# A two-layer graph-attention kernel: which queue stores the transposed rows in the first scores and the sums of h in the first aggregate

## The chip, the cores and the metric

The kernel runs on one core of a Trainium2 chip, as one program with one launch. The metric is the device time of a whole execution in microseconds (us). A core has five engines that run at once, each with its own instruction stream: TensorE (PE, matrix products), VectorE (DVE), ScalarE (ACT), GpSimd (POOL) and SyncE (SP). They wait for one another through semaphores. A transfer (DMA) between the chip's memory and on-chip memory is issued by an instruction on one of these streams and then carried out by 16 DMA engines that all streams share.

## The reference

Two layers of graph attention work on 2708 rows of 1024 values in fp32. `adj`, 2708 x 2708 integers, says which pairs of rows count.

```python
h = jnp.maximum(_layernorm(x, axis=-1), 0.0)
# layer 0
f = h @ Wf + bf
g = h @ Wg + bg
e = jax.nn.relu(f @ g.T)
scores = jnp.where(adj > 0, e, NEG)
attention = jax.nn.softmax(scores, axis=1)
x = x + attention @ (h @ W + bW)
# layer 1, on the h of the new x
h1 = h @ W1
e = jax.nn.leaky_relu(h1 @ a1 + (h1 @ a2).T, negative_slope=0.2)
attention = jax.nn.softmax(jnp.where(adj > 0, e, neg), axis=1)
x = x + jax.nn.relu(attention @ h1)
```

Only layer 0 is touched here: its scores (the argument of the softmax) and its product of the attention with h.

## The kernel before, in words

**Tiles.** The rows of h are taken in 21 tiles of 128 rows and a small rest. Twenty tiles form ten pairs, numbered 0 to 9; pair q holds tiles 2q and 2q+1. The rest is a left-over unit. The output rows are worked on in five panels of some 512 columns, numbered 0 to 4. "First" scores and "first" aggregate mean those of panel 0 in layer 0.

**Products in seven parts.** Large products are done two by two blocks at a time with seven products (M1 to M7) in place of eight. That takes sums and differences of the blocks beforehand. The left operand of the scores is h transposed, so for each pair the kernel keeps eight tiles of 128 x 512 of transposed rows: four straight from transposing and four sums of these. The right operand of the aggregate's side is h itself, again with sums of its blocks.

**The order of stages.** First a product of the weights, M = Wf Wgᵀ (line 591), while x is loaded, normalised and transposed (`make_pairs`, from line 441). Then `project_q(0)`, which makes the right sides B of the first scores, then `scores(0, B)`, then `project_q(1)` with the softmax of panel 0 beside it, then `aggregate(0, 0, ...)`, then `project` and the next panel. So TensorE does long products while VectorE and ScalarE prepare the next ones.

**Work in between.** Preparing steps are put on a list with an estimated time each (`put`, line 201). The stages call `behind(us)` at fixed places between their products, which takes steps off the list as long as their credit lasts. The steps are written into the program at that place, so their order is fixed when the program is built. VectorE is held in program order in the scores, SyncE's loads (`load`, line 137) and ScalarE's transfers through `by_scalar` (line 545) everywhere; the other instructions are ordered by a scheduler.

**The transposed rows.** For one pair, `transposes` (line 464) transposes on TensorE into psum banks; ScalarE copies four of them to four buffers `ts`, called hsT, each two tiles long (512 KB). `sums` (line 478) makes the other four tiles on VectorE, in the order M5, M6, M7, M3, and then stores the four buffers to `hs_d[q]` in the chip's memory. The store is `store` (line 141), a DMA issued by GpSimd. The buffers' order is that of `BY_SCORES` (line 31): M1 with M6, M5 with M2, M7 with M3, M4 with the last. Each store waits for the sum that lies in its buffer.

**The first scores.** `scores(p, B)` (line 1399) goes over the ten pairs q. At the start of each, `make_until(q + 2)` sees to it that pair q + 2 has been made, so that the last pairs are transposed, summed and stored while TensorE works on earlier ones; in the first scores these are pairs 7, 8 and 9 for the stores. Then `fetch(q + 3)` issues the loads of a later step's part of `adj` (tiles adj_i and, for panel 0's 64 extra columns, adj_t). `product` (line 1415) loads the left operands As from `hs_d[q]` with SyncE, two of the seven at a time, and multiplies them (line 1424). M4 of a pair comes only after the first product of the next pair, through `left_over`. VectorE adds up what TensorE leaves in psum (sx, sy, sz), and TensorE needs these banks again.

**The buffers.** hsT, As, adj_i, the tiles of h for sums (hr), and many more (hc, weights) all come from one pool, `strm`, of 12 buffers of 512 KB. A buffer is given out again when its last user is done. For an hsT buffer, that is its store to hs_d.

**The first aggregate.** `rows_h` (line 368) stores a pair's h to `hg_d`; later `sums_h` (line 376) loads it back (hr), makes the sums M5, M7, M6 and M3 on VectorE in two steps, and stores them to `hg_d` again, in three stores. Some pairs' sums are made before the aggregate, the others in it; `sums_until(NQ)` after product M4 makes the rest. The loads are ScalarE's or SyncE's. The aggregate (line 678) goes over its products in the order M1, M2, M4, M5, M6, M3, M7, and ScalarE copies what M1 left in psum (gx) to on-chip tiles.

**Completion semaphores.** In the built program, DMAs that SyncE and ScalarE issue report to eight completion semaphores, taken in turn in the order in which the program was written; GpSimd's report to eight others. A DMA that takes a semaphore carries a wait for the last DMA on it.

**Another transfer in that time.** `columns_to_row` (line 272) turns a few columns of r into a row in the chip's memory, `r_d` for panels 1 to 4 (called at the end of the first panel's loop body, but issued by GpSimd as soon as r is there).

Of the kernel before, what the change touches and what calls it, by code (L numbers as in the profile page):

```python
# [25 lines left out]
M1, M5, M6, M7, M3, M2, M4 = range(7)  # L26
# [31 lines left out]
def kernel(  # L58
# [82 lines left out]
    def store(o, i):  # L141
        for a, b in in_16(o, i):
            nc.gpsimd.dma_start(a, b)  # L143
# [9 lines left out]
    hs_d = [dram.tile([P, 8, NH, P], FP, name=f"hs_d{q}") for q in range(NQ)]  # L153
# [3 lines left out]
    hg_d = [dram.tile([P, 7, len(g), W], FP, name=f"hg_d{i}") for i, g in enumerate(groups)]  # L157
# [39 lines left out]
    later, lazy, credit = [], [], [0.0]  # L197
    ahead = [5]
    spare, from_slots = [False], [False]

    def put(us, go, fetch=None, takes_psum=False, ready=None, to=later):
        to.append([us, fetch, go, takes_psum, ready])
# [168 lines left out]
        for m, h in ((M1, ha[0]), (M5, ha[1]), (M2, hb[0]), (M4, hb[1])):  # L371
            store(hg_d[i][:, m, j], h)

    summed, sums_may = [0], [True]

    def sums_h():

        def fetch(q, two):
            i, j = group_of[q]
            for m in (M1, M2):  # L380
                two.append(stream("hr", (P, 2, W)))
                (load if "m" in got else by_scalar)(two[-1], hg_d[i][:, m:m + 2, j])

        def first(q, two):
            (a0, a1), (b0, b1) = ((t[:, 0], t[:, 1]) for t in two)
            add(b1, a1, b1)
            sub(a1, a0, a1)

        def second(q, two):
            (a0, a1), (b0, b1) = ((t[:, 0], t[:, 1]) for t in two)  # L390
            sub(a0, b1, a0)
            sub(b0, b0, a0)
            i, j = group_of[q]
            store(hg_d[i][:, M6:M7 + 1, j], two[0])
            store(hg_d[i][:, M3, j], b0)
            store(hg_d[i][:, M5, j], b1)
            summed[0] += 1
        for q in range(NQ):
            two = []
            put(1.4, lambda q=q, two=two: held(first, q, two), lambda q=q, two=two: fetch(q, two), ready=lambda: sums_may[0])  # L400
            put(1.4, lambda q=q, two=two: held(second, q, two), ready=lambda: sums_may[0])
# [39 lines left out]
    def make_pairs():  # L441
        xs, hT = {}, {}

        def fetch(q):
            xs[q] = []
            for t in units[q]:
                xs[q].append(row_halves("x"))
                load_rows_of(t, xs[q][-1], x)

        def rows(q):  # L450
            left_h(0, *xs[q]) if q == LEFT else rows_h(q, *xs[q])

        def turned(q, k, e):
            t = units[q][k]
            ps = bank("h_ps", (P, NH, P))
            for c in range(NH):
                nc.tensor.transpose(ps[:, c, :], xs[q][k][e][:, c * P:(c + 1) * P], ident)
            for i, (s, n) in enumerate(pieces[0]):
                if s == t:
                    o = first_h[e].rearrange("p (c i) -> p c i", c=NH)[:, :, i * P:i * P + n]  # L460
                    nc.vector.tensor_copy(o, ps[:, :, :n])
            return ps

        def transposes(q):
            if q == LEFT:
                two = stream("hsl", (P, 2, NH, P))
                for e in range(2):
                    nc.scalar.copy(two[:, e], turned(q, 0, e))
                    nc.scalar.copy(tinyT[:, e], turned(q, 1, e)[:, :, :B32])
                store(hsl_d.rearrange("p e c j -> p (e c j)"), two.rearrange("p e c j -> p (e c j)"))  # L470
            else:
                ts = [stream("hsT", (P, 2, NH, P)) for _ in range(4)]
                hT[q] = ts, lambda i: ts[i // 2][:, i % 2]
                for k, e, i in ((0, 0, 0), (0, 1, 3), (1, 0, 7), (1, 1, 6)):
                    nc.scalar.copy(hT[q][1](i), turned(q, k, e))
            turned_tiles.update(units[q])

        def sums(q):
            if q == LEFT:
                return  # L480
            ts, i = hT.pop(q)
            at = {m: i(k) for k, m in enumerate(BY_SCORES)}
            add(at[M5], i(7), at[M4])
            sub(at[M6], at[M5], at[M1])
            sub(at[M7], at[M1], i(7))
            sub(at[M3], at[M2], at[M6])
            for g, t in enumerate(ts):
                store(hs_d[q][:, 2 * g:2 * g + 2].rearrange("p m c j -> p (m c j)"), t.rearrange("p m c j -> p (m c j)"))

        def dots(q, k):  # L490
            t = units[q][k]
            c = col_of[t]
            dot(r_[:, c:c + 1], xs[q][k], [vb[e][:, :W] for e in range(2)], c0)
            if t == MONO:
                nc.gpsimd.dma_start(r_[:NM, HALF:HALF + 1], r_[NM:, c:c + 1])

        def drop(q, what):
            seen.setdefault(q, set()).add(what)
            if len(seen[q]) == 3:
                xs.pop(q)  # L500

        def last(q):
            sums(q)
            drop(q, "sums")
            made.add(q)

        def bias(q, k):
            dots(q, k)
            drop(q, f"dots{k}")

        seen = {}
        def put_norms(q):
            put(2.1, lambda: normalize(xs[q][0]), lambda: fetch(q))
            put(2.1, lambda: normalize(xs[q][1]))

        put_rows = lambda q: put(0.5, lambda: rows(q))
        def put_dots(q):
            for k in range(2):
                put(1.6, lambda k=k: bias(q, k), ready=lambda: vb[0] is not None)

        todo = [0, 1, LEFT] + list(range(2, NQ))
        put_norms(todo[0])
        for i, q in enumerate(todo):
            if i + 1 < len(todo):
                put_norms(todo[i + 1])
            put_rows(q)
            put(0.5, lambda q=q: transposes(q), takes_psum=True)
            if i > 1:
                put_dots(q)
            put(2.7 if q != LEFT else 0.0, lambda q=q: last(q))  # L530
            if i == 1:
                put_dots(todo[0])
                put_dots(todo[1])
# [117 lines left out]
    for name, gs in (("pick_lo", (0, 1)), ("pick_hi", (0, 2, 3))):  # L651
        t = consts.tile([P, P], FP, name=name)
# [746 lines left out]
    def scores(p, B):  # L1399
# [46 lines left out]

        nc.hold = ("vector",)
        left_over = None
        for q in range(NQ):
            n = P  # L1450
            make_until(q + 2)
            rate = 1.3 if NQ - 1 not in made else rates[p]
            if q + 3 <= LEFT:
                fetch(q + 3)
            if p == 0 and q == NQ - 2:
                ahead[0] = 2
                sums_h()
            if p in ORDERED and q in (2, 6):
                (copy_residual if q == 2 else bias_residual)(p)
            sa, sb = slot("Sa"), slot("Sb")  # L1460
            S[pairs[q][0]], S[pairs[q][1]] = sa, sb
            X, Y, Z = (bank(f"s{k}") for k in "xyz")
            m1, t = slot("sm1"), slot("st")
            product(q, M1, X, True)
            for s in (lo, hi):
                add(m1[:n, s], X[:n, :h], rb[:n, s])
            if left_over:
                left_over()
            product(q, M6, Z, True)
            add(t[:n, lo], Z[:n, :h], m1[:n, hi])  # L1470
            behind(rate, True)
            product(q, M5, Y, True)
            add(t[:n, hi], Y[:n, :h], m1[:n, hi])
            if q + 2 <= LEFT:
                convert(q + 2, p > 0)
            behind(rate, True)
            product(q, M2, X, False)
            add(sa[:n, lo], X[:n, :h], rb[:n, lo])
            if q + 2 <= LEFT:
                turn(q + 2, 0)  # L1480
            behind(rate, True)
            product(q, M7, Z, False)
            add(sb[:n, hi], Z[:n, :h], t[:n, hi])
            if q + 2 <= LEFT:
                turn(q + 2, 1)
            behind(rate, True)
            product(q, M3, Y, False)
            add(sa[:n, hi], Y[:n, :h], t[:n, lo])
            finish(q, sa, 0)
            behind(2 * rate, True)  # L1490
            left_over = lambda q=q, sb=sb, Z=Z, m1=m1: last(q, sb, Z, m1)
# [6 lines left out]
        t = stream("As", (P, 2, NH, P))  # L1498
# [268 lines left out]
    for p in range(NP):  # L1767
# [16 lines left out]
        if p == NP - 2:  # L1784
            then[M2] = lambda: first_masks(NP - 1, 0)
            then[M6] = lambda: first_masks(NP - 1, 1)
            then[M7] = lambda: first_masks(NP - 1, 2)
        spare[0], from_slots[0] = p > 0, p == NP - 1
        G[p] = aggregate(0, p, S, got["sm"], then)
        spare[0] = False  # L1790
        if p == 0:
# [115 lines left out]
    for p in range(NP):  # L1907
# [6 lines left out]
        g = aggregate_quartered(p, S, sm, next_right, then, fine=1.0) if p else aggregate(1, p, S, sm, then, rate=4.0)  # L1914
# [34 lines left out]
```

## Time and profile before

| what | value |
|---|---|
| median of 3 runs | 3050.46 us (3048.57 to 3051.97) |
| the profiled execution: its own time | 3055.39 us |
| its span, from the first to the last instruction | 3053.6 us |
| mean granted TensorE clock, of full speed | 0.995 |
| TensorE busy | 2999.1 us |
| VectorE, ScalarE, GpSimd busy | 2048.9, 536.5, 495.2 us |
| matmuls of the scores (line 1424), all panels | 2800 |

The profile is of one execution; its time is not that of the median run, and sums made from its durations are to be set against its own. A group of the page is a line and an operation with its output and inputs, such as `sx<-B,As`; after the count come the busy time in us and the mean of one in ns, and last the idle time of the engine just before these instructions with what ended most of it. A timeline has the start in us from the span's start, the length, the engine, line and operation, how many instructions, and in brackets the idle time before the first one and what ended it. `SPq` is SyncE's queue, where a DMA's issue with its waits is seen as an instruction.

### The profile page before, as it was taken

The numbers are of one execution on the slowest core, as the hardware profiler recorded it, in microseconds if no ns is written. First come the engines' busy times: TensorE is split into PE (matmuls) and PEld (weight loads), VectorE is DVE, ScalarE is ACT, GpSimd is POOL, SyncE is SP. The second block draws the span as 40 slices with busy tenths as digits, with TensorE's granted clock in tenths as the row PEclk, the third lists the DMA queues.
The fourth block names the chain that finished last, engine by engine and source line by source line (L and its number), as shares of the span: only waits on it lengthen the run. The fifth ranks groups of instructions, "written<-read, shape, count | busy, mean of one in ns | idle before, by whom it ended". The sixth has DMA issues, their size and how long they took to land.

```text
span 3053.6 us, 41717 instructions
## 1 busy us (share of the span) xinstructions
PE 2999.1 (98%) x14642; PEld 2300.7 (75%) x14642; DVE 2048.9 (67%) x4667; ACT 536.5 (18%) x880; POOL 495.2 (16%) x770
## 2 busy tenths in 40 slices
PE   8998999999999999999999999999999999999999
PEld 4576777667877588885888886784767959879695
DVE  5776794585742686616965376867878768887863
ACT  3420020020200221101220111202232131212200
POOL 1421111210112110223101111131212010020201
PEclk9999999999999999999999999999999999999999
DMA  6989978887466785768957587678757768878797
GB/s 228 303 271 269 313 277 308 268 281 235 131 236 164 233 271 192 245 156 258 291 186 251 176 244 252 238 293 324 257 190 265 260 200 298 292 266 296 258 302 267
DMA packets 392704, 766.78 MB, mean 251 GB/s; under 512 B 65728, under 2 KB 206944, under 8 KB 392464
## 3 DMA queue, kind: packets, MB, share of 16 engines
q1 hardware_dynamic: 332336, 584.80, 59.4%
q0 software_dynamic: 54464, 164.78, 16.1%
q10 hardware_dynamic: 5696, 14.55, 1.4%
q8 instruction: 116, 1.90, 0.2%
q14 instruction: 92, 0.75, 0.1%
HBM read 630.04 MB, written 138.11 MB: 252 GB/s over the span
## 4 chain that ended last, share of the span: by engine, by line
PE 70%; issue 12%; DVE 11%; DMA 4%; POOL 2%; ACT 1%; SPq 0%; POOLq 0%; DVEq 0%; ACTq 0%
PE gy L678 6%; PE gz L678 6%; PE sz L1424 5%; PE gz L1113 5%; PE gx L678 5%; PE pz L1313 4%; PE px L1313 4%; PE sy L1424 3%; PE sx L1424 3%; PE gx L1113 3%; PE M_ps L591 3%; PE py L1313 3%; PE gy L1113 3%; PE gv L678 3%; DVE P L45 2%
## 5 line engine op out<-in xcount | busy, mean ns | idle before, releaser
L1424 PE MATMUL sz<-B,As 128*128 128x288 f32 (+2 forms) x1200 | 292.9, 393 | 5.4 <-DVE st L45 5.2
L1424 PEld LDWEIGHTS sz<-B,As 128*128 128x128 f32 x1200 | 228.3, 191 | 54.5 <-DVE st L45 8.4
L1424 PE MATMUL sx<-B,As 128*128 128x288 f32 (+2 forms) x800 | 201.3, 395 | 11.0 <-DMA As<-hs_d 9.3
L1424 PE MATMUL sy<-B,As 128*128 128x288 f32 (+2 forms) x800 | 199.0, 392 | 0.0
L1424 PEld LDWEIGHTS sx<-B,As 128*128 128x128 f32 x800 | 152.8, 192 | 44.0 <-DMA As<-hs_d 9.7
L678 PE MATMUL gz<-Sa,hc 128*128 128x288 f32 (+2 forms) x800 | 185.8, 393 | 0.0
L678 PEld LDWEIGHTS gz<-Sa,hc 128*128 128x128 f32 x800 | 151.7, 190 | 32.0 <-issue 2.2
L1424 PEld LDWEIGHTS sy<-B,As 128*128 128x128 f32 x800 | 152.0, 190 | 30.4 <-DVE st L45 0.3
L1113 PE MATMUL gz<-quarter,hc 128*128 128x128 f32 (+2 forms) x1344 | 168.9, 279 | 3.8 <-DVE gT L45 3.7
L1113 PEld LDWEIGHTS gz<-quarter,hc 128*128 128x128 f32 x1344 | 160.6, 191 | 5.1 <-DVE gT L45 4.6
L143 POOL DMA_DIRECT2D out_dram<-x_res x164 | 81.0, 500 | 469.1 <-DVE x_res L45 463.1
L1313 PE MATMUL py<-w,ps 128*128 128x512 f32 x320 | 142.1, 593 | 0.0
L1313 PE MATMUL pz<-w,ps 128*128 128x512 f32 x320 | 142.0, 595 | 0.0
L1313 PE MATMUL px<-w,gT 128*128 128x512 f32 x320 | 141.1, 593 | 0.0
L678 PE MATMUL gy<-T,hc 128*128 128x288 f32 (+2 forms) x480 | 115.0, 402 | 3.8 <-DMA hc<-hg_d 3.8
L1313 PEld LDWEIGHTS pz<-w,ps 128*128 128x128 f32 x320 | 60.3, 190 | 76.2 <-issue 72.1
L1313 PEld LDWEIGHTS py<-w,ps 128*128 128x128 f32 x320 | 60.6, 190 | 75.0 <-issue 72.6
L591 PE MATMUL M_ps<-wgT,wfT 128*128 128x512 f32 x256 | 112.7, 597 | 1.6 <-ACT hsT L45 1.6
L1313 PEld LDWEIGHTS px<-w,gT 128*128 128x128 f32 x320 | 60.2, 190 | 71.2 <-issue 67.8
L678 PEld LDWEIGHTS gy<-T,hc 128*128 128x128 f32 x480 | 93.2, 194 | 24.6 <-DMA hc<-hg_d 4.3
L143 POOL DMA_DIRECT2D mk_d<-mask x55 | 35.9, 652 | 455.6 <-DVE mask L45 427.3
L45 ACT ACTIVATE P<-P 128x576 f32<-128x576 f32 (+3 forms) x111 | 72.1, 650 | 207.3 <-DVE P L45 207.3
(391 smaller groups left out, 5829.0 us busy)
## 6 DMA issues: line engine op xcount, KB each, us to landing
hc<-hg_d SPq DMA_DIRECT2D x175, 512.0 KB
As<-hs_d SPq DMA_DIRECT2D x150, 512.0 KB
hc<-hr_d SPq DMA_DIRECT2D x119, 512.0 KB
hc<-hs_d SPq DMA_DIRECT2D x112, 512.0 KB
w<-wt_d SPq DMA_DIRECT2D x96, 512.0 KB
w<-in_L_gnn_W_dram SPq DMA_DIRECT2D x72, 512.0 KB
md<-md_d SPq DMA_DIRECT2D x56, 512.0 KB
adj_i<-in_adj_dram SPq DMA_DIRECT2D x200, 128.0 KB
```

The lines of the kernel that those rows point to most:

```text
L45: i = f(*a, **k)
L143: nc.gpsimd.dma_start(a, b)
L591: nc.tensor.matmul(ps, wfT[a][c // NH][:, c % NH, :], wgT[b][c], start=(c == 0), stop=(c == NC - 1))
L678: nc.tensor.matmul(ps[d], left(m, k, d), right(m, k), start=(start and k == 0), stop=(k == K - 1), skip_group_check=True)
L1113: nc.tensor.matmul(ps[:, d], lhs[:, d * P:(d + 1) * P], inner_right(m, n, k), start=(start and k == 0 and d == 0), stop=(k == NK - 1), ski ...
L1313: nc.tensor.matmul(ps, left[i][m][:, k, :], w_[k], start=(start and k == 0), stop=(k == NH - 1), skip_group_check=True)
L1424: nc.tensor.matmul(ps[:n, :h], lefts[q][:, i % 2, c, :n], B[m][c // 2][:, c % 2, :h], start=(start and c == 0), stop=(c == NH - 1), skip_g ...
```

## The change

A flag `by_act` is set at the start of `scores`: true for panel 0, false for the later panels. Where it is true, the four stores of a pair to `hs_d` go out by `by_scalar`, that is, from ScalarE's queue in program order, and not by `store` from GpSimd's. A flag `in_first` is set just ahead of an aggregate of layer 0: true for panel 0. Where it is true, the three stores of a pair's sums of h to `hg_d` go out by `by_scalar` as well. The order of these three is also changed, for all pairs: M5 goes first, then M6 with M7, then M3.

```diff
     spare, from_slots = [False], [False]
+    by_act = [False]
...
-    summed, sums_may = [0], [True]
+    summed, sums_may, in_first = [0], [True], [False]
...
             i, j = group_of[q]
-            store(hg_d[i][:, M6:M7 + 1, j], two[0])
-            store(hg_d[i][:, M3, j], b0)
-            store(hg_d[i][:, M5, j], b1)
+            out = by_scalar if in_first[0] else store
+            out(hg_d[i][:, M5, j], b1)
+            out(hg_d[i][:, M6:M7 + 1, j], two[0])
+            out(hg_d[i][:, M3, j], b0)
             summed[0] += 1
...
             for g, t in enumerate(ts):
-                store(hs_d[q][:, 2 * g:2 * g + 2].rearrange("p m c j -> p (m c j)"), t.rearrange("p m c j -> p (m c j)"))
+                (by_scalar if by_act[0] else store)(hs_d[q][:, 2 * g:2 * g + 2].rearrange("p m c j -> p (m c j)"),
+                                                    t.rearrange("p m c j -> p (m c j)"))
...
         left_over = None
+        by_act[0] = p == 0
         for q in range(NQ):
...
         spare[0], from_slots[0] = p > 0, p == NP - 1
+        in_first[0] = p == 0
         G[p] = aggregate(0, p, S, got["sm"], then)
```

## The prediction

> **What bounds the kernel now.** I read the page's busy shares first, then the groups for what TensorE waited for, then the timelines of TensorE, SP, GpSimd, ScalarE and VectorE around that wait. The page:
>
> ```profile
> span 3053.6 us, 41717 instructions
> PE 2999.1 (98%) x14642; PEld 2300.7 (75%) x14642; DVE 2048.9 (67%) x4667; ACT 536.5 (18%) x880; POOL 495.2 (16%) x770
> L1424 PE MATMUL sx<-B,As 128*128 128x288 f32 (+2 forms) x800 | 201.3, 395 | 11.0 <-DMA As<-hs_d 9.3
> L678 PE MATMUL gy<-T,hc 128*128 128x288 f32 (+2 forms) x480 | 115.0, 402 | 3.8 <-DMA hc<-hg_d 3.8
> ```
>
> TensorE is busy for 2999.1 of 3053.6 us, so an edit off it is worth what TensorE's waits lose or gain. The stages that the change touches hold two: 9.3 us in the first scores, 3.8 us in the first aggregate. TensorE's timeline places the first (start, length, work, idle before it):
>
> ```profile
> 236.47 2.10 PE L1424 MATMUL sy<-B,As 128*128 128x288 f32 x8
> 247.86 4.21 PE L1424 MATMUL sx<-B,As 128*128 128x288 f32 x8 [9.29 <-DMA As<-hs_d]
> 251.86 5.02 PE L1424 MATMUL sz<-B,As 128*128 128x288 f32 x16
> ```
>
> Pair 2 starts 9.29 us late, and its first two groups take 9.2 us where others take 2.10 and 4.04: 3.1 us more. SP's timeline says why the load came late:
>
> ```profile
> 210.81 13.96 SPq L139 DMA_DIRECT2D As<-hs_d  x4
> 236.39 2.06 SPq L139 DMA_DIRECT2D adj_i<-in_adj_dram  x4
> 238.49 2.86 SPq L139 DMA_DIRECT2D adj_t<-in_adj_dram  x4
> 241.47 10.18 SPq L139 DMA_DIRECT2D As<-hs_d  x4
> ```
>
> SP stands from 224.8 to 236.4, before adj_i; its longest wait here, 11.5 us, is for an hs_d store, which frees the adj_i buffer. GpSimd, VectorE and ScalarE (timelines), and issue to landing (DMA view):
>
> ```profile
> 216.56 0.54 POOL L143 DMA_DIRECT2D hs_d<-hsT  x1 [2.47 <-ACT hsT L45]
> 220.41 0.76 POOL L275 DMA_DIRECT2D r_d<-r  x1 [3.32 <-DVE r L45]
> 225.91 1.60 POOL L143 DMA_DIRECT2D hs_d<-hsT  x3 [4.74 <-DVE Sa L45]
> ```
> ```profile
> 222.40 2.58 DVE L45 TENSOR_TENSOR hsT<-hsT 128x512 f32<-128x512 f32 x4
> ```
> ```profile
> 214.21 2.05 ACT L45 COPY hsT<-h_ps 128x512 f32<-128x512 f32 x4 [0.95 <-PE h_ps L457]
> 228.24 0.29 ACT L45 ACTIVATE rs<-mv,eps 128x1 f32<-128x1 f32 x1 [11.97 <-DVE mv L45]
> ```
> ```profile
> r_d<-r POOLq DMA_DIRECT2D x1, 2.0 KB, 9.1
> hs_d<-hsT POOLq DMA_DIRECT2D x3, 512.0 KB, 9.9
> ```
>
> Pair 7's sums end at 223.1, 223.8, 224.4 and 225.0. GpSimd issues their stores behind r_d[...]: r_d takes 9.1 us to land, the stores after it 9.9, an SP load issued at 224.45 landed at 233.69 (semaphore events), while the store ahead of it, at 216.56, took 5.6.
>
> [...]
>
> **The change part by part.** The instruction order is the same on TensorE, VectorE and SP. Of the stores only the last are moved: pairs 7, 8 and 9 in the scores (12 stores of 512 KB), and sums 7, 8 and 9 in the aggregate (9 stores). The others went out before the switch or come from the sums made ahead.
>
> Issue: GpSimd loses 21 x 0.54 = 11 us; it is 16% busy and sets nothing, so 0. ScalarE gains 21 issues of 0.37 (its hr loads' row): 8 us. For pair 7 they fall into its idle 11.97 us: 0.
>
> The wait that is added is not in the diff. SP's and ScalarE's DMAs take eight completion semaphores in turn, and a DMA waits for the last one on its semaphore to land. Pair 7's four stores come in between SP's loads, so in the built program:
> - pair 0's last As load (for M4, issued at 211.42 before) waits for pair 7's first store, and pair 1's third for the second;
> - adj_t for step 5, just ahead of pair 2's first As load, waits for pair 8's first two stores;
> - pair 3's first As load waits for pair 9's first store.
> SP is in order, so all behind stands too. Each time a load needed now waits for a store of sums that VectorE makes later.
>
> *First wait.* ScalarE's first store needs the second sum, so 223.9. It meets r_d: landing bounds 5.6 and 9.9 us from the rows above; I take 8: 231.9. The 256 KB load to its first matmul: bounds 4 and 6.4 (247.86 - 241.47 for 512 KB in a crowd); I take 5: 236.9. TensorE wants it at 225.0, after pair 1's first group. Wait 11.9 (8.5 to 15).
>
> *Second wait.* TensorE's rest of pair 1 takes 238.6 - 225.0 = 13.6, plus 3.1 slow: ready for pair 2 at 253.6. VectorE, in order, has the add of pair 0's M4 at 229.62 and pair 8's sums at 243.08: 13.5 us of work. That add can come at 236.9 + 4.2 = 241.1, so pair 8's sums start at 254.6, the second ends at 255.9. Store 4.6 us to landing (as the quiet one issued at 259.70), 1.3 for the second store, 0.6 for the issues left: pair 2's load at 262.4. 5.5 to the matmul (bounds 5 and 6.4): 267.9. Wait 14.3, where 9.3 was.
>
> *Third wait.* Pair 2 runs 266.23 - 247.86 = 18.4: ready at 286.3. Pair 9's second sum ended 17.7 after pair 2's start (264.23 + 1.3 - 247.86): 285.6. The next r_d falls beside it, so landing 4.6 to 10.8, taken 7: 292.6; load 5.5: 298.1. Wait 11.8, then 3.1 slow.
>
> Sum: pair 3 starts at 298.1 where it started at 266.23: +31.9; with the slow start +35. Low ends together give +24, high ends +44. From there TensorE is bound by itself, and nothing gives it back; loads that run ahead meanwhile may save 0 to 4 us in later waits, I take 2: +33.
>
> *Aggregate.* ScalarE now waits for the sums of pairs 7 and 8 ahead of its four copies of M1, from which M2 goes on in the same banks. The last of these sums ends at 446.8, its issue at 447.2; the first copy was at 447.20 and TensorE started M2 at 449.92. So +0.1, and 2.3 us of cover; past that it costs one for one. Pair 9's stores come after the copies. The 3.8 us wait is for a load that follows wt_d stores, which are not moved: 0. Reversing the order of the three stores changes one pair on GpSimd's queue: 0.
>
> On the profiled execution's own 3053.6 that is 3087; its run took 3055.39, 0.16% over the median, so I add the 33 to the median: 3050.5 + 33 = 3083.5.
>
> **The rivals.**
> 1. *One wait for one.* Only the first wait is real; in it VectorE and the queues catch up, so pairs 8 and 9 store in time. Then 11.9 + 3.1 replaces 9.3 + 3.1: +3, 3053. For: the wait removed is on the same stores. Against: VectorE's 13.5 us chain starts only with pair 0's M4, after the wait. Two waits of the three, near 3068, lies between.
> 2. *The stores escape.* Free of GpSimd's queue and r_d, pair 7's stores land early, SP's 11.5 us go, and 9.3 + 3.1 is gained: 3038. It is decided at one place: pair 0's M4 load must be issued before about 219.5 (225.0 - 5.5). The sums end at 223.8, which speaks against it, unless SP doesn't wait as built.
> 3. *ScalarE holds TensorE in the aggregate*, on top of the three waits: if the sums come over 2.3 us later against TensorE than now; perhaps 6 us, 3090.
>
> **How the numbers follow.** Three waits 0.74, own range 3070 to 3096; two waits 0.08; one for one 0.08; escape 0.06; aggregate too 0.04. The measurement tells 0.2%, 6 us, from no change: faster 0.06, same 0.07 (nearly all of rival 1), slower 0.87. The range leaves out the escape, one for one, and the tails: 3059 to 3097.
>
> **What would show it.** Right: in the first scores three TensorE waits of about 12, 14 and 12 us for As, ahead of pair 0's M4 (sz), pair 2 and pair 3; SP waiting longest for hs_d stores just ahead of As loads; GpSimd's DMA count down by 21, with no gain; the 3.8 us wait unchanged. Wrong: pair 0's M4 load still issued near 211, TensorE without idle at 225, or M2 of the first aggregate late behind ScalarE's copies.

## The result and the profile after

The changed kernel takes 3086.71 us (median of 4 runs, 3083.30 to 3089.29) against 3050.57 for the kernel before (median of 4: the three runs above and one more): 1.0118 times as long, 95% interval 1.0105 to 1.0131, or 36 us more. The forecast was 3083.5 us, with a range of 3059 to 3097.

The page of the changed kernel's profile; its lines have moved by up to three, so that the scores' line 1424 is 1427 and the aggregate's 678 is 681:

```profile
span 3082.1 us, 41685 instructions
PE 2996.5 (97%) x14642; PEld 2295.6 (74%) x14642; DVE 2048.6 (66%) x4667; ACT 536.9 (17%) x880; POOL 485.6 (16%) x749
L1427 PE MATMUL sz<-B,As 128*128 128x288 f32 (+2 forms) x1200 | 294.4, 395 | 17.6 <-DMA As<-hs_d 12.2
L1427 PE MATMUL sx<-B,As 128*128 128x288 f32 (+2 forms) x800 | 203.0, 397 | 31.9 <-DMA As<-hs_d 30.2
```

TensorE does the same 14642 matmuls in 2.6 us less of busy time. Its waits for As have grown from 9.3 to 42.4 us. The wait of the first aggregate for hg_d (the group gy<-T,hc) is what it was, 3.6 us (before 3.8). GpSimd has 21 instructions fewer (749 in place of 770), which are the 21 stores moved. TensorE's timeline says where the 42.4 us are (start, length, work, and in brackets the idle time ahead of it and what ended it):

```profile
237.56 5.76 PE L1427 MATMUL sz<-B,As 128*128 128x288 f32 x16 [12.21 <-DMA As<-hs_d]
...
268.38 3.78 PE L1427 MATMUL sx<-B,As 128*128 128x288 f32 x8 [15.56 <-DMA As<-hs_d]
...
300.16 4.21 PE L1427 MATMUL sx<-B,As 128*128 128x288 f32 x8 [14.61 <-DMA As<-hs_d]
```

There are three waits: at 225.4, ahead of the group that holds pair 0's M4; at 252.8, ahead of pair 2; at 285.6, ahead of pair 3. Pair 3, which began at 266.23 before, begins at 300.16. Behind each wait the first group is slow: 3.78 and 4.21 us where eight matmuls take 2.10, and 5.76 where sixteen take 4.04. The TensorE clock granted in the trace was 0.50 of full speed from 230.6 to 240.9, from 257.9 to 271.6 and from 288.7 to 305.7, that is, in the later part of each wait and in the start behind it, and 1.00 in between. In the kernel before it was 0.50 from 243.6 to 253.8, about its one wait in this stage. ScalarE's and SP's timelines show the other side, the four stores of a pair and the loads that stand for them:

```profile
224.02 2.79 ACTq L45 DMA_DIRECT2D hs_d<-hsT  x4
258.18 2.78 ACTq L45 DMA_DIRECT2D hs_d<-hsT  x4
284.85 2.77 ACTq L45 DMA_DIRECT2D hs_d<-hsT  x4
```
```profile
215.19 18.71 SPq L139 DMA_DIRECT2D As<-hs_d  x4
...
241.71 21.70 SPq L139 DMA_DIRECT2D adj_t<-in_adj_dram  x4
...
265.44 7.16 SPq L139 DMA_DIRECT2D adj_i<-in_adj_dram  x4
294.88 2.48 SPq L139 DMA_DIRECT2D As<-hs_d  x4
```

The 18.71 us of the first row hold one load issued at 215.19 and three from 232.56 on: SP stood between them. It stood again from 242.0 inside adj_t, until 260.8, and from 272.6 to 294.9 behind adj_i. Its waits (who waited for what: us in all, times, the longest), taken from 200 to 320 us:

```profile
SPq L139 <- DMA hs_d<-hsT: 59.6, 5, 22.2
```

The trace's semaphore events give the landing of the first store of pairs 7, 8 and 9 as 232.50, 260.78 and 294.82; SP goes on at 232.56, 260.80 and 294.88. Each time the load goes within 0.06 us of the landing. In all three cases the semaphore that the load waits for is the one to which it then reports its own landing, and to which the store reported: it is the shared turn, and not a buffer, that ends the wait. In this trace SyncE's 1899 transfers and ScalarE's 61 report to the same eight semaphores, and GpSimd's 707 to eight others; before, ScalarE had 40 and GpSimd 728.

### The profile page after: what moved, and what is told of

Its sections match the earlier page's. It is cut to its first block, busy times and chain, and to the rows that moved or that the text cites. A ratio compares the mean times of both kernels' runs of the same rounds, so it can differ in the third digit from the quotient of the medians.

```text
span 3082.1 us, 41685 instructions
## 1 busy us (share of the span) xinstructions
PE 2996.5 (97%) x14642; PEld 2295.6 (74%) x14642; DVE 2048.6 (66%) x4667; ACT 536.9 (17%) x880; POOL 485.6 (16%) x749
## 4 chain that ended last, share of the span: by engine, by line
PE 73%; issue 12%; DVE 10%; DMA 3%; POOL 1%; SPq 1%; ACT 1%; POOLq 0%; DVEq 0%; ACTq 0%
PE gy L681 7%; PE gz L681 6%; PE gx L681 6%; PE sz L1427 5%; PE gz L1116 5%; PE pz L1316 4%; PE px L1316 4%; PE sx L1427 3%; PE sy L1427 3%; PE py L1316 3%; PE gy L1116 3%; PE gx L1116 3%; PE M_ps L594 3%; PE gv L681 3%; PE qz L681 3%
## 5 line engine op out<-in xcount | busy, mean ns | idle before, releaser
L1427 PE MATMUL sz<-B,As 128*128 128x288 f32 (+2 forms) x1200 | 294.4, 395 | 17.6 <-DMA As<-hs_d 12.2
L1427 PE MATMUL sx<-B,As 128*128 128x288 f32 (+2 forms) x800 | 203.0, 397 | 31.9 <-DMA As<-hs_d 30.2
```

Source lines behind the costliest of these rows:

```text
L1427: nc.tensor.matmul(ps[:n, :h], lefts[q][:, i % 2, c, :n], B[m][c // 2][:, c % 2, :h], start=(start and c == 0), stop=(c == NH - 1), skip_g ...
```

## The experiments

Each run's ratio is to the kernel before, timed alongside it on the same chip, with its 95% interval in brackets. "Drift" below is how much later a matmul starts than the same one in the profile of the kernel before; the order of matmuls is the same in all these kernels. Where a drift has a time, it is the matmul's time in the kernel before.

**The two halves apart.** The first run keeps the stores of the sums of h as they were, and moves the transposed rows alone:

```diff
-            out = by_scalar if in_first[0] else store
-            out(hg_d[i][:, M5, j], b1)
-            out(hg_d[i][:, M6:M7 + 1, j], two[0])
-            out(hg_d[i][:, M3, j], b0)
+            store(hg_d[i][:, M6:M7 + 1, j], two[0])
+            store(hg_d[i][:, M3, j], b0)
+            store(hg_d[i][:, M5, j], b1)
```

> Only the stores of the transposed rows (hs_d, pairs 7, 8 and 9) go by ScalarE's queue; the stores of the sums of h are those of before. Theory (SP's loads wait, through the completion semaphores that SP and ScalarE share, for the stores): everything is here, three TensorE waits of about 12, 15.5 and 14.5 us for As, ahead of pair 0's M4, pair 2 and pair 3, and the time of the whole change, 3087 us (3082 to 3091). Rival (ScalarE holds TensorE in the first aggregate): some 6 us less than the whole change, 3080.

Measured: 3089.64 us, 1.0121 (1.0106 to 1.0136), waits of 12.4, 14.6 and 14.4 us. The second run is the other half:

```diff
-        by_act[0] = p == 0
+        by_act[0] = False
```

> Only the stores of the sums of h in the first aggregate go by ScalarE's queue, in the new order; the transposed rows are stored as before. Theory: 3050.5 us as before (3047 to 3054), one As wait of 9.3 us in the first scores, and M2 of the first aggregate with less than 1 us of idle ahead of it. Rival (ScalarE's in-order queue holds the copies of M1): 3 to 8 us over before, with idle time of TensorE at M2.

Measured: 3052.16 us, 1.0009 (1.0000 to 1.0018). One wait for As of 9.7 us. ScalarE's timeline at the turn from M1 to M2 of the first aggregate, and TensorE's:

```profile
441.36 8.09 ACTq L45 DMA_DIRECT2D hg_d<-hr  x6
```
```profile
439.79 12.53 PE L681 MATMUL gx<-Sa,hc 128*128 128x288 f32 x51
452.16 4.04 PE L681 MATMUL gx<-Sb,hc 128*128 128x288 f32 x16
```

The six stores of sums 7 and 8 are out at 449.45, just before TensorE has the first bank ready, and M2 (the row of Sb) starts without a gap. TensorE's drift is 2.2 us ahead of this place and behind it. So all of the loss is in the transposed rows, and the aggregate's half, which has the new order of the three stores too, costs about nothing.

**The place in the count, without the data.** All stores stay on GpSimd. ScalarE issues, beside each, a transfer of 512 bytes out of the same buffer to scratch memory:

```diff
                 store(hs_d[q][:, 2 * g:2 * g + 2].rearrange("p m c j -> p (m c j)"), t.rearrange("p m c j -> p (m c j)"))
+                if by_act[0]:
+                    by_scalar(tiny_d[q][:, g], t[:1, 1, 0])
```

> All stores are those of before, by GpSimd. Beside each of the four stores of pairs 7, 8 and 9 ScalarE issues one transfer of 512 bytes, out of the same buffer into scratch memory that nothing reads. It has the place in the program that the moved store had, and waits for the same sum. Theory (the semaphores couple SP's loads to the sums): three TensorE waits for As come up, at pair 0's M4, pair 2 and pair 3, each shorter by what 512 bytes land sooner than 512 KB: about 8, 12 and 9 us, 3075 us (3066 to 3084). Rival (it is the moved stores' own data, sharing the DMA engines with the loads in another order): as before, 3050.5, with one wait of 9.3.

Measured: 3084.90 us, 1.0104 (1.0089 to 1.0119). TensorE's timeline and SP's waits from 200 to 320 us:

```profile
236.07 6.87 PE L1428 MATMUL sz<-B,As 128*128 128x288 f32 x16 [9.32 <-DMA As<-hs_d]
...
266.47 4.21 PE L1428 MATMUL sx<-B,As 128*128 128x288 f32 x8 [14.03 <-DMA As<-hs_d]
...
297.88 4.21 PE L1428 MATMUL sx<-B,As 128*128 128x288 f32 x8 [12.92 <-DMA As<-hs_d]
```
```profile
SPq L139 <- DMA tiny_d<-hsT: 51.2, 5, 22.9
```

No 512 KB store was moved, and 3084.9 - 3050.8 = 34.1 of the 36 us are there. SP waits 51.2 us for twelve transfers that carry 6 KB in all and write what nobody reads. That is the coupling and not the data: what the loads need is not in what they wait for. The rival falls. The time lies 10 us above the estimate and just outside its range, because the three waits came out at 9.3, 14.0 and 12.9 us rather than 8, 12 and 9. The reason for the last: the small transfer for pair 9 was issued at 284.21, beside an r_d store of 282.12, and the load that waits for it went only at 293.63.

**The stores later in the program.** The four stores of a pair are kept back and written after the next pair's M7 load:

```diff
+                stores.append((at_pair[0], put_out)) if by_act[0] else put_out()
...
             product(q, M7, Z, False)
+            while stores and stores[0][0] < q:
+                stores.pop(0)[1]()
```

> The whole change, but a pair's four hs_d stores are written into the program later: after the load for M7 of the next pair, so that in the built program pair 0's M4 load and pair 1's third load stand ahead of pair 7's stores and carry no wait for them. Pair 9's first store still lies eight transfers ahead of pair 3's first load. Theory: no wait at pair 0's M4; at pair 2 a wait of about 5 us where before had 9.3 (adj_t ahead of it waits for all four of pair 7's stores); the wait of some 12 us at pair 3 stays: 3059 us (3052 to 3066). Rival (ScalarE's issuing of these stores, or their data, is what holds TensorE, wherever they stand): as the whole change, 3087.

Measured: 3072.13 us, 1.0067 (1.0050 to 1.0084). TensorE's timeline, then ScalarE's:

```profile
224.55 4.04 PE L1428 MATMUL sz<-B,As 128*128 128x288 f32 x16
...
249.21 4.21 PE L1428 MATMUL sx<-B,As 128*128 128x288 f32 x8 [11.11 <-DMA As<-hs_d]
...
281.99 3.62 PE L1428 MATMUL sx<-B,As 128*128 128x288 f32 x8 [14.75 <-DMA As<-hs_d]
```
```profile
232.65 0.29 ACT L45 ACTIVATE rs<-mv,eps 128x1 f32<-128x1 f32 x1 [2.66 <-DVE mv L45]
233.43 0.81 ACT L45 ACTIVATE x<-x,rs 128x512 f32<-128x512 f32 x1 [0.48 <-DVE rs L45]
233.96 0.34 ACTq L45 DMA_DIRECT2D hs_d<-hsT  x1
```

Pair 0's M4 (the first row, sixteen matmuls) starts at once: no wait where no store stands eight transfers ahead. At pair 3, where one still does, the wait is 14.75 us. So it is the place in the program that decides, and not ScalarE as the issuer; the theory holds at both ends. The 11.1 us at pair 2, in place of 5, is why the time lies above its range. What it had wrong is when pair 7's stores go: their sums are there at 224, but, written later, the stores stand in ScalarE's program behind a normalisation that waits for VectorE's moments until 232.65, and the first was issued at 233.96.

**One pair at a time.** Three runs move the stores of one pair only, with the sums of h stored as before:

```diff
-                (by_scalar if by_act[0] else store)(hs_d[q][:, 2 * g:2 * g + 2].rearrange("p m c j -> p (m c j)"),
+                (by_scalar if by_act[0] and q == 7 else store)(hs_d[q][:, 2 * g:2 * g + 2].rearrange("p m c j -> p (m c j)"),
```

> Only pair 7's four hs_d stores go by ScalarE's queue; pairs 8 and 9 and the sums of h are stored as before. Theory: the wait of 12 us at pair 0's M4 comes, but it takes the place of the 9.3 us wait at pair 2, which falls away since pair 7's stores land in it, and neither pair 2 nor pair 3 waits for a store: about 3054 us (3050 to 3060). Rival (each of the three waits costs its own 12 to 15 us on top of what was there): 3064.

Measured: 3064.29 us, 1.0039 (1.0026 to 1.0052). A wait of 12.44 us at pair 0's M4; TensorE's timeline after it:

```profile
252.64 2.10 PE L1426 MATMUL sx<-B,As 128*128 128x288 f32 x8
...
266.09 2.18 PE L1426 MATMUL sz<-B,As 128*128 128x288 f32 x8 [1.84 <-DMA As<-hs_d]
...
272.25 2.21 PE L1426 MATMUL sx<-B,As 128*128 128x288 f32 x8 [2.04 <-DMA As<-hs_d]
...
280.92 2.99 PE L1426 MATMUL sy<-B,As 128*128 128x288 f32 x8 [2.58 <-DMA As<-hs_d]
```

The first wait does take the place of the one at pair 2, which starts at 252.64 with no idle time ahead; by the start of pair 2's second product the drift is down to 2.0 us. But then come three waits of 1.84, 2.04 and 2.58 us that were not expected. VectorE makes pair 8's sums only after the add behind the first wait, at 256.66 in place of 243.08, so GpSimd's stores of pairs 8 and 9 come later against TensorE than before: SP's load behind the first of them goes at 260.67, just after that store landed (260.54). The drift is 11.7 us at 514 us. The time is the rival's, the waits are not: the 9.3 us were not kept.

The same edit with `q == 8`:

> Only pair 8's four hs_d stores go by ScalarE's queue. Theory: no wait at pair 0's M4 and none at pair 3; the load ahead of pair 2 waits for pair 8's first two stores, whose sums are made at 243 to 244.4 as before, so the store lands near 249, the load goes at 252, and pair 2 starts near 257 in place of 247.9: one wait of some 18 us where 9.3 was, 3060 us (3056 to 3064). Rival (without the first wait pair 8's sums are early enough): 3050.5, one wait of 9 to 10.

Measured: 3059.75 us, 1.0020 (1.0009 to 1.0030). No wait at pair 0's M4 nor at pair 3, and one of 15.57 us at pair 2; the stores were issued at 245.47 and the load at 250.84:

```profile
255.05 4.21 PE L1426 MATMUL sx<-B,As 128*128 128x288 f32 x8 [15.57 <-DMA As<-hs_d]
```

And with `q == 9`:

> Only pair 9's four hs_d stores go by ScalarE's queue. Theory: the 9.3 us wait at pair 2 stays, and pair 3's first load, which stands eight transfers behind pair 9's first store, brings a new wait of some 13 to 15 us with a slow start after it: 3067 us (3062 to 3071). Rival (the third wait is only the echo of the first one, through VectorE): 3050.5, no new wait.

Measured: 3066.58 us, 1.0041 (1.0026 to 1.0056). TensorE's timeline:

```profile
276.94 3.99 PE L1426 MATMUL sx<-B,As 128*128 128x288 f32 x8 [14.31 <-DMA As<-hs_d]
```

The wait at pair 3 stands on its own and is 14.3 us, as with the whole change; it is no echo. (The wait at pair 2 was 4.6 us and not 9.3 in this execution. Pair 7's three stores, behind r_d as before, landed in 6.1 to 8.7 us where the profile before has 9.1 to 10.6; why is not known.) The three pairs cost 0.39, 0.20 and 0.41% alone, 1.00% together, against 1.21% for all three moved with the sums of h stored as before.

**The r_d stores out of the way.** r_d was blamed for the late stores of the kernel before and for part of the landing times. Here its columns are copied by VectorE after the first aggregate, and r_d is stored from the copy:

```diff
             for s in range(1, NP):
-                columns_to_row(r_d[s], s, r_[:, first_col[s]:])
+                for n, i, j in [(P, 0, F)] + [(n, F, F + 1) for _, n in pieces[s][F:]]:
+                    held(nc.vector.tensor_copy, r_late[:n, first_col[s] + i:first_col[s] + j],
+                         r_[:n, first_col[s] + i:first_col[s] + j])
+                columns_to_row(r_d[s], s, r_late[:, first_col[s]:])
```

> The kernel before, but the columns of r are copied after the first aggregate and r_d is stored from the copy, so that its small pieces don't lie among pair 7's and pair 9's stores. Theory (the 9.3 us wait of before is GpSimd's stores standing behind r_d and landing beside it): pair 7's three stores are issued by 225 and land by 231, the wait at pair 2 shrinks to 0 to 3 us without a slow start: 3041 us (3037 to 3046). Rival (the stores are late for VectorE's sums and the crowd of loads): 3050.5, wait over 7.

Measured: 3060.43 us, 1.0031 (1.0023 to 1.0038), slower, where 3041 was expected and the rival had no change. GpSimd's timeline and TensorE's:

```profile
224.34 0.54 POOL L143 DMA_DIRECT2D hs_d<-hsT  x1 [6.25 <-DVE hsT L45]
```
```profile
239.83 2.21 PE L1424 MATMUL sx<-B,As 128*128 128x288 f32 x8 [0.26 <-DMA As<-hs_d]
...
636.59 3.78 PE L1313 MATMUL pz<-w,gT 128*128 128x512 f32 x4 [4.67 <-DVE x_res L45]
```

The first part held: pair 7's three stores go as soon as the sums are there, at 224.34, 225.06 and 226.27, and land in 2.9 to 5.9 us, the 9.29 us wait is 0.26, and TensorE is 10.9 us ahead at 254 us. Smaller waits take some of that back, and at 590 us 4.9 of them are left. Then the six r_d stores, now issued from 587.5 on among the loads of the first project, take 11.4 to 16.0 us to land, and TensorE waits there for a load of weights (2.6 us), for pt (1.6) and for x_res (4.7, the second row above), where the kernel before has none of these waits: at 638 it is 8.6 us behind. On GpSimd's own eight semaphores there was one wait of that kind too: a load for x_res that it issued at 599.88 had waited for the first r_d store, which landed at 599.60 on the semaphore that the load takes. How much of TensorE's loss comes from that wait is not shown.

The same edit on the changed kernel:

> The whole change, with r_d stored late as in the run without the change. Theory: the three waits stay, for they hang on the sums, but the stores of pairs 7 and 9 land in some 5 us and not in 8 to 12: waits of about 9, 15 and 10 us, 3079 us (3073 to 3085), so that against the kernel before with r_d late the change costs more, not less: some 38 us. Rival (r_d is what makes the moved stores costly): waits under 5 us, below 3065.

Measured: 3092.62 us, 1.0130 (1.0114 to 1.0146); waits of 7.2, 15.6 and 8.2 us, close to what was expected, and the loss in the first project on top, which was not: 7.6 us above the range given. Against the run before it, the change costs 32 us.

The next pair of runs leaves the r_d stores of panels 1 and 2 where they were and moves those of panels 3 and 4, which lie in the first scores, to a quieter place, after the scores of panel 1:

```diff
+        if p == 1:
+            r_late = consts.tile([P, 2 * F], FP, name="r_late")
+            held(nc.vector.tensor_copy, r_late, r_[:, first_col[3]:first_col[3] + 2 * F])
+            for s in range(3, NP):
+                columns_to_row(r_d[s], s, r_late[:, (s - 3) * F:])
...
-            for s in range(1, NP):
+            for s in range(1, 3):
```

> The kernel before, with only the two r_d stores that lie in the first scores moved, to a stretch with few transfers (from about 790 us on), out of a copy of their columns of r. Theory: the first scores gain what they gained with all of r_d late (7 us at pair 3), and the 18 us that were lost again in the first project, where r_d then lay among loads, don't come back: 3044 us (3038 to 3049). Rival (the gain is taken back by later waits wherever r_d goes): 3051 or more.

Measured: 3045.09 us, 0.9981 (0.9969 to 0.9992). This is about 6 us faster than the kernel before, by its interval 2 to 9. The stores of r_d were issued at 788.6 and 789.4. In TensorE's timeline the wait at pair 2 is down to 0.98 us, and two of 1.74 and 1.14 us come after it:

```profile
242.53 2.21 PE L1424 MATMUL sx<-B,As 128*128 128x288 f32 x8 [0.98 <-DMA As<-hs_d]
```

And this edit on the changed kernel:

> The whole change with the same two r_d stores moved to the same place. Theory: three waits as with all of r_d late (7, 15.5 and 8 us), pair 3 some 24 us later than before, and no new loss in the first project: 3075 us (3068 to 3081), still over 25 us above the kernel without the change and with r_d moved. Rival (without r_d the change is free): within 6 us of it.

Measured: 3081.77 us, 1.0100 (1.0080 to 1.0120), with the same three waits (7.2, 14.8 and 8.2 us), 0.8 us above the range given. Against the run just before it the change costs 36.7 us between the medians, as much as with r_d in its old place, but 26.6 us between the two profiled executions, nearer to what the waits in these two traces account for (30.2 us for As against 3.9). So r_d made the first and the third wait longer (12.2 and 14.6 us in the whole change), but it isn't what makes the change slow; how much of the 36 us it adds is left open by these two figures.

## Why the prediction was right

**The added wait.** The step on which all rested, that SP's loads would wait for ScalarE's stores through the semaphores that both take in turn, held, and was shown three times: by the semaphores in the trace, by 512-byte transfers in the same places, which alone bring 34 us, and by writing the stores later, which takes away the one wait that then has no store eight transfers ahead.

**The three waits.** Forecast 11.9, 14.3 and 11.8 us; found 12.2, 15.6 and 14.6.
- First: landing of the store forecast 231.9, found 232.5; first matmul 236.9, found 237.6. The 8 us taken for a landing beside r_d were 8.5.
- Second: TensorE ready at 253.6, found 252.8. Pair 8's sums were to start at 254.6 and started at 256.7, since 15.3 us lay between the late add (241.41) and the sums where 13.5 were taken, 1.8 of them a wait of VectorE for TensorE. The landing was quicker (2.6 us, 4.6 taken). First matmul 267.9, found 268.4: the two errors, 2 us each, cancel, so that this forecast came so close is luck.
- Third: the sums were in time (second one at 284.7, forecast 285.6). The term that was mis-sized is the landing beside r_d: 10.0 us, where 7 was taken between 4.6 and 10.8. First matmul 298.1, found 300.2.

The slow start after each wait was taken as 3.1 us, from the one in the kernel before; it was 1.7, 1.7 and 2.8, from the starts of the groups behind it. The clock of 0.50 lasted 3.3, 3.2 and 5.5 us past the end of the three waits, where it lasted 5.9 in the kernel before, and half of such a stretch is what it costs: 1.7, 1.6, 2.8 and 3.0 us. That every new wait would cost 3.1 was the author's estimate. Pair 3 came 33.9 us later (31.9 forecast), and 36.8 with the slow start after it (35).

**What comes back later.** 2 us were taken off. Between the two profiles the drift is 37.0 us at 374 us, and they end 28.5 us apart, so some 8 us come back, 4.6 of them at 2202 us: the profiled execution of the kernel before has a wait of 2.63 us there, with a granted clock of 0.50 from 2202.8 to 2206.2, that the profile after lacks. But that execution took 4.8 us more than the median of its kernel, and the other 2.0 us less than the median of its own. The medians differ by 36.1 us, about the drift of the first scores. If that drift is the same in the other executions, which have no trace, nothing comes back in the median. The forecast was 3 us low in all: 1.8 in the first scores, the rest about the 2 us taken off.

**The aggregate.** Forecast +0.1 us at the first copy of M1: it came at 484.21, which is 37.0 us later than before, as is TensorE at that time, so nothing was added, and M2 had no gap. The half alone measures 0 to 0.18%.

**The rivals.** "One wait for one" was wrong for the whole change, but it is what pair 7's stores do alone up to pair 2's second product, where the drift is 2.0 us; the waits after that brought it to 11.7. The first wait gives VectorE's later sums no time to catch up, since they come after an add that is itself behind the wait. "The stores escape" fell at the place it named: pair 0's M4 load was issued at 232.56, and not before 219.5. It was right in one thing, though, that r_d is what costs the kernel before most of its 9.3 us: without it the wait is 0.3 to 1.0 us, with two smaller ones after it.

## What to carry to other kernels

Before a transfer is given to another queue, ask which counters the queues share. Here SyncE and ScalarE took eight completion semaphores in turn, and SyncE's in-order loads waited for ScalarE's transfers eight places ahead: 59.6 us in five waits for the stores of 512 KB, and 51.2 us in five waits for the transfers of 512 bytes that nobody reads. The diff doesn't show this; the waits of the built program do. And before curing a late store, look at what was issued just ahead of it: here the cure was to move two r_d stores of 2 KB to a stretch with little traffic (a DMA share of 0.37 from 780 to 820 us in the kernel before), and where they were put decided whether that gained some 6 us or lost some 9.

## What the runs showed of the hardware that was not expected

ScalarE's queue issued a transfer ahead of its own unfinished work: in the run with the later stores four copies of pair 8 stand ahead of the first store in the program, and yet the store was issued at 233.96, within a normalisation that ran for 0.81 us from 233.43, and the first of the copies began at 234.85. Here the store was held back by the wait in front of it, until 232.65, and not by the copies there.

Size said little about how long others waited for a transfer at pair 9: 512 bytes beside an r_d store held the load behind them for 9.4 us (284.21 to 293.63), and 512 KB in the same place took 10.0 us to land. At pair 7, also beside r_d, size did count: 3.3 us (225.37 to 228.69) against 8.5. And how long r_d itself took to land differed by place: 9.1 and 10.1 us in the first scores of the kernel before, 14.1 (median of the four of 2 KB) among the loads of the first project.
